# GpSimd and VectorE in program order: a two-layer graph kernel with its planner's order taken from two engines

## The chip, the cores and the metric

The kernel runs on one core of a Trainium2 chip. The core has four compute engines, each with an instruction queue that it works through in order: TensorE (PE in the profile) for matrix products, VectorE (DVE), ScalarE (ACT) and GpSimd (POOL). SyncE (SP) issues most of the DMAs. Engines wait for one another through semaphores. The metric is the time of one execution on the device in microseconds.

## The reference

A graph of 2708 nodes with 128 features and an adjacency matrix `adj` of which most entries are zero, since each node has a few neighbours and itself; each row is scaled to sum to 1. Two layers follow each other, each added to its input and normalized:

```python
x = _layernorm(x + _L0_gnn_ref(x, adj, W))       # hyperbolic mean over neighbours
x = _layernorm(x + _L1_gnn_ref(x, adj, ...))     # messages between neighbours

# layer 0
XW = mobius_matvec(W, X)
gamma = 2.0 / jnp.maximum(1.0 - jnp.sum(XW * XW, axis=-1, keepdims=True), EPS)
two_mean = (A_hat @ (gamma * XW)) / _clamp_abs(A_hat @ (gamma - 1.0))
...                                               # norms, artanh, tanh, relu
# layer 1
messages = gelu(s[:, None, :] + d[None, :, :] + msg_b)
aggregated = jnp.einsum('ijd,ij->id', messages, adj)
new_feats = concatenate([node_feats, aggregated]) @ upd_w.T + upd_b
h = gelu(new_feats) + node_feats                  # then a layer norm with ln_w, ln_b
```

Layer 0 needs products with the whole adjacency matrix. Layer 1 needs a gelu for each edge of the graph.

## The kernel before, in words

Nodes are cut into 22 blocks of 124 rows. The kernel goes through the following work, most of it overlapped.

**Products.** For each block, two halves of its adjacency columns are loaded (`aT`, L372, issued by SP). ACT turns them into signs (L375), DVE checks them against the diagonal (L378), and TensorE multiplies the signs with the prepared features (L397). DVE evacuates the sums (L413) and searches the packed words of the same product for the places of the neighbours (L431, L433). The sums stand in one of two PSUM banks called "op".

**Batches.** Blocks are grouped into seven batches. A batch turns the places into lists of edges: peeling the keys (L451 to L454), sorting (L493), counting (L506 to L527), places from a product with a triangular matrix (TensorE L523 and L524, DVE L536), a running sum (L538), a split into three parts that goes back and forth between ACT and DVE (L547, ACT L550, L554, ACT L555, L558), one-hot rows `R` (ACT L566, DVE L569), a selection by TensorE (L583), and the index `J` of the neighbour for each edge (L591 to L599).

**Epilogues.** Blocks are also grouped into five chunks (0 to 4, 5 to 8, 9 to 13, 14 to 18, 19 to 21). For a chunk, a chain of small DVE operations computes the factors of layer 0: L630, a power on POOL (L632), L641 to L669 with a logarithm and a tanh on ACT, then residual and statistics (L679 to L682), L685, a second power on POOL (L145), L689. Then each block is normalized (ACT L697, POOL L700), transposed (L702) and projected (L708, L709, into an "op" bank). The projection is written to a table in HBM (L716) and split into parts (ACT L315 and L317, DVE L316 and L318). Table 0 holds blocks 0 to 8, table 1 the others.

**Messages.** POOL gathers the neighbour's row from the table for 128 edges at a time (L342, an indirect DMA, four of them to a group `dd`, five groups buffered). DVE adds the own part (L765), ACT applies gelu (L766), TensorE sums by node (L778). A first pass uses table 0 (66 gathers), a second pass table 1 (41 gathers). In the second pass each finished block is updated (L817, L818, ACT L819), and groups of one to four blocks are normalized twice (`finish`: L828, L807 to L809, power on POOL L145, L834, L838, statistics and power again, L846, ACT L848) and stored.

**What sets the order.** The Python code does not emit stage after stage. The main loop over blocks emits loads, products and evacuations; beside it stand "threads", lists of small steps of batches, epilogues and the first message pass, each with a start and an end on a clock of blocks. After every main step `advance` emits the steps of each thread that have become due. The second message pass emits finish steps through `queue` and `drain`, one step of messages at a time. What is emitted is then handed to the scheduler of the language, which orders the instructions of each engine by its own estimate of when they are ready, taking the emission order as a priority. Each engine then issues in the order that results.

Of the kernel before, what the change touches and what calls it, by code (L numbers as in the profile page):

```python
# [10 lines left out]
F32 = mybir.dt.float32  # L11
U32 = mybir.dt.uint32
BF16 = mybir.dt.bfloat16
I32 = mybir.dt.int32
AF = mybir.ActivationFunctionType
OP = mybir.AluOpType
# [49 lines left out]
def hyperbolic_then_message_kernel(  # L66
# [148 lines left out]
    def cols(n, pool=sc, p=Q):  # L215
        count[0] += 1
        name = f"c{count[0]}" if count[0] < 100 else "k" + SHORT[count[0] - 101]
        return pool.tile([p, max(n, NB)], F32, name=name)[:, :n]
# [90 lines left out]
    def bank(name, bufs=2):  # L309
        return ps.tile([P, 512], F32, name=name, bufs=bufs)  # L310
# [51 lines left out]
    def signs_of(b):  # L362

        def load():
            dgb = stream.tile([P, Q], F32, name="dgb", bufs=2)
            nc.sync.dma_start(dgb, bass.AP(tensor=adj_r.tensor, offset=adj_r.offset + b * Q, ap=[[0, P], [1, Q]]))
            signs[b] = (stream.tile([Q, NB, Q], BF16, name="sgn"), dgb)

        def half(h):
            sgn, dgb = signs[b]  # L370
            aP = stream.tile([P, HALF, Q], F32, name="aT", bufs=3)
            nc.sync.dma_start(aP, adj_t[b, :, h * HALF : (h + 1) * HALF, :])  # L372
            aT = aP[:Q]
            at = 2 * b + h
            nc.scalar.activation(  # L375
                sgn[:, h * HALF : (h + 1) * HALF, :], aT.bitcast(U32), AF.Sign, accum_out=nn[:, at : at + 1]
            )
            nc.vector.scalar_tensor_tensor(  # L378
                aT,
                aT,  # L380
                1.0,
                dgb[:Q].unsqueeze(1).to_broadcast([Q, HALF, Q]),
                op0=OP.mult,
                op1=OP.is_equal,
                accum_out=ne[:, at : at + 1],
            )

        return [load, lambda: half(0), lambda: half(1)]

    def products(b):  # L390

        def part(j0, j1):
            if j0 == 0:
                sums[b] = bank("op")
            op, (sgn, _) = sums[b], signs[b]
            for j in range(j0, j1):
                nc.tensor.matmul(  # L397
                    op[:Q, :WIDE], lhsT=sgn[:, j, :], rhs=ym[:, j, :], start=(j == 0), stop=(j == NB - 1)
                )
                if j == 0:  # L400
                    nc.tensor.matmul(
                        op[:Q, KEYS:WIDE], lhsT=nidentb[:Q, :Q], rhs=ym[:, b, KEYS:], start=False, stop=False
                    )

        return [lambda: part(0, HALF), lambda: part(HALF, NB)]

    def evacuate(b):

        blocks, S = of_block[b]

        def first():
            op = sums[b]
            nc.vector.tensor_reduce(  # L413
                nom[:, b, :], op[:Q, :ONES].rearrange("p (g d) -> p d g", g=3), axis=AX.X, op=OP.add
            )
            nc.scalar.copy(cnt[:, b : b + 1], op[:Q, ONES : ONES + 1])  # L416
            if b == blocks[0]:
                if S:
                    v = small.tile([Q, len(blocks), S, 8], F32, name="v", bufs=2)
                    idx = small.tile([Q, len(blocks), S, 8], U32, name="idx", bufs=2)  # L420
                    slots[blocks] = (v, idx)
                else:
                    words = small.tile([Q, Q], F32, name="words")
                    nc.scalar.copy(words, op[:Q, KEYS:WIDE])
                    slots[blocks] = (words, None)
            if S:
                v, idx = slots[blocks]
                i = b - blocks[0]
                words = op[:Q, KEYS:WIDE]
                for s, (lo, hi) in enumerate(segments(S)):  # L430
                    nc.vector.max(v[:, i, s, :], words[:, lo:hi])  # L431
                for s, (lo, hi) in enumerate(segments(S)):
                    nc.vector.max_index(idx[:, i, s, :], v[:, i, s, :], words[:, lo:hi])  # L433

        def second():
            u = nom[:, b, :D]
            junk = row.tile([Q, D], BF16, name="junk")
            nc.scalar.activation(junk, u, AF.Square, accum_out=ss[:, b : b + 1])
            nc.scalar.activation(u, u, AF.Relu)
            junk = row.tile([Q, D], BF16, name="junk")  # L440
            nc.scalar.activation(junk, u, AF.Square, accum_out=us[:, b : b + 1])

        return [first, second]
# [369 lines left out]
    def update(agT, b, dgb):  # L813

        h = own1[:, b, :]
        up = bank("sel", SELS)
        nc.tensor.matmul(up[:Q, :D], lhsT=agT, rhs=wu2, start=True, stop=True)  # L817
        nc.vector.scalar_tensor_tensor(h, up[:Q, :D], dgb, h, op0=OP.mult, op1=OP.add)  # L818
        nc.scalar.activation(h, h, AF.Gelu)  # L819
# [104 lines left out]
    def advance(now):  # L924
        for t in threads:
            start, end, steps, done = t
            due = len(steps) if now >= end else int(len(steps) * max(0.0, now - start) / (end - start))
            while t[3] < due:
                steps[t[3]]()
                t[3] += 1  # L930
# [21 lines left out]
        thread(clock, clock + n * PACE, messages(0, range(b0, b1), kept))  # L952
        clock += n * PACE

    for i in range(NB + 1):
        main = []
        if i == 1:
            main.append(lambda: nc.sync.dma_start(x_all, x_p))
        if i < NB:
            main += signs_of(i)  # L960
        if i >= 1:
            main += products(i - 1)
            main += evacuate(i - 1)
        for k, step in enumerate(main):
            step()
            advance(i + (k + 1) / len(main))
    now = NB + 1.0
    late_at = max(t[1] for t in threads)
    while now < late_at:
        now = min(late_at, now + 0.05)  # L970
        advance(now)

    count[0] = 60
    bad = cols(4, p=Q)
    bp = bank("sel", SELS)
    nc.tensor.matmul(bp[:Q, :NL], lhsT=ones[:Q, :Q], rhs=deg, start=True, stop=True)
    over = cols(NL)
    nc.vector.tensor_tensor(over, bp[:Q, :NL], cap, op=OP.is_gt)
    nc.vector.tensor_reduce(bad[:, 0:1], over, axis=AX.X, op=OP.max)
    dz = cols(NB)  # L980
    cn = cols(4)
    nc.vector.tensor_scalar(dz, dg, 0.0, None, op0=OP.is_le)
    nc.vector.tensor_reduce(cn[:, 0:1], dz, axis=AX.X, op=OP.add)
    nc.vector.tensor_reduce(cn[:, 1:2], nn, axis=AX.X, op=OP.add)
    nc.vector.tensor_reduce(cn[:, 2:3], ne, axis=AX.X, op=OP.add)
    nc.vector.tensor_reduce(cn[:, 3:4], deg, axis=AX.X, op=OP.add)
    cp = bank("sel", SELS)
    nc.tensor.matmul(cp[:Q, :4], lhsT=ones[:Q, :Q], rhs=cn, start=True, stop=True)
    tot = cols(4)
    nc.scalar.copy(tot, cp[:Q, :4])  # L990
    pads = float(NP - N)
    nc.vector.tensor_scalar(bad[:, 1:2], tot[:, 0:1], pads, None, op0=OP.not_equal)
    nc.vector.tensor_scalar_add(tot[:, 2:3], tot[:, 2:3], -pads * NP)
    nc.vector.tensor_tensor(bad[:, 2:3], tot[:, 2:3], tot[:, 1:2], op=OP.not_equal)
    nc.vector.tensor_scalar_add(tot[:, 3:4], tot[:, 3:4], float(N))
    nc.vector.tensor_tensor(bad[:, 3:4], tot[:, 3:4], tot[:, 1:2], op=OP.not_equal)
    bsum = cols(1)
    nc.vector.tensor_reduce(bsum, bad, axis=AX.X, op=OP.add)
    flag = sc.tile([Q, 1], I32, name="flag")
    nc.vector.tensor_copy(flag, bsum)  # L1000

    queue = []
    groups = []
    at = 0
    for n in ENDS:
        groups.append(LATE_ORDER[at : at + n])
        at += n
    group_of = {b: g for g in groups for b in g}
    state = {}

    def ended(b, ag, at):
        agT = edge.tile([P, Q], F32, name="agT", bufs=4)
        nc.scalar.copy(agT, ag[:, :Q])
        bs = group_of[b]

        def up():
            update(agT, b, dg[:, b : b + 1])

        queue.append((at + 1, up))
        if b == bs[-1]:  # L1020
            for k in range(3):
                queue.append((at + 2 + k, lambda k=k: state.setdefault((bs[0], "f"), finish(bs))[k]()))

    def drain(now):
        due = [q for q in queue if q[0] <= now]
        queue[:] = [q for q in queue if q[0] > now]
        for _, f in due:
            f()

    for i, step in enumerate(messages(1, LATE_ORDER, ended)):  # L1030
        step()
        drain(i - (DDS - 2))
    drain(10**6)

    dense = nc.values_load(flag[0:1, 0:1], min_val=0, max_val=4)
    with tc.If(dense > 0):
# [123 lines left out]
```

## Time and profile before

| what | us |
|---|---|
| median of 3 runs | 466.12 (463.27 to 473.36) |
| the profiled execution, its own time | 462.5 |
| span of the profiled execution | 460.7 |
| DVE busy | 280.5 |
| PE busy | 278.5 |
| ACT busy | 233.8 |
| POOL busy | 175.8 |
| first gather from table 0 starts at | 185.85 |
| first gather from table 1 starts at | 360.32 |

A row of the timeline gives start and length in microseconds, the engine, the line of the kernel, the operation, output and inputs, shapes, and in brackets the idle time of the engine before it with what ended that time. "x3" merges neighbours of a kind. A row of the waits reads: engine, line and tile that waited, what it waited for, total microseconds, number of times, longest case. The names of tiles leave out buffer numbers.

### The profile page before, as it was taken

The page shows a single profiled execution, that of the slowest core. Times are in us where ns is not written, and L with a number is a line of the kernel's source. Part 1 is how long each engine was busy: PE and PEld are TensorE (multiplying, and loading weights), DVE is VectorE, ACT ScalarE, POOL GpSimd, SP SyncE. Part 2 cuts the span into 40 slices and gives each one's busy share as a digit, 9 for nine tenths or more (in the row PEclk, how much of TensorE's full clock was granted, in tenths as well). Part 3 has the DMA queues.
Part 4 walks back from the last instruction along what each step waited for, and adds up shares of the span by engine and source line. Part 5 has one row for each costly group of instructions (what it writes and reads, how often), then busy time and mean ns, then how long its engine had stood idle before and what let it go on. Part 6 is the DMA issues. An engine that isn't in the chain of part 4 may idle for free. (4 is left out here: it accounts for less than half of the span.)

```text
span 460.7 us, 6392 instructions
## 1 busy us (share of the span) xinstructions
PE 278.5 (60%) x1813; PEld 198.2 (43%) x1813; DVE 280.5 (61%) x1174; ACT 233.8 (51%) x647; POOL 175.8 (38%) x332
## 2 busy tenths in 40 slices
PE   3606948471789328966509578987089767556500
PEld 3603525240356114645308445855046656555400
DVE  3896898989717892355138553679286223338770
ACT  3764646366546756434028565677178333233520
POOL 9900000020401001677770770012724777782230
PEclk9855997975589858977758969999589896865755
DMA  7970444353234660163512351830100222121110
GB/s 185 369 192 1 127 126 130 82 174 127 67 90 162 159 187 23 43 234 112 175 43 74 102 144 36 207 110 11 46 25 24 62 52 53 48 55 40 37 33 15
DMA packets 20160, 45.86 MB, mean 100 GB/s; under 512 B 6185, under 2 KB 12517, under 8 KB 19861
## 3 DMA queue, kind: packets, MB, share of 16 engines
q1 hardware_dynamic: 15413, 37.75, 27.1%
q0 software_dynamic: 3424, 7.02, 6.0%
q10 hardware_dynamic: 1280, 0.60, 0.7%
q8 instruction: 16, 0.26, 0.3%
q14 instruction: 27, 0.22, 0.2%
HBM read 42.58 MB, written 2.78 MB: 98 GB/s over the span
## 5 line engine op out<-in xcount | busy, mean ns | idle before, releaser
L342 POOL DMA_INDIRECT dd<-table_dram,J x107 | 109.5, 1023 | 60.6 <-issue 27.9
L397 PE MATMUL op<-ym,sgn 124*124 124x512 bf16 x484 | 122.7, 407 | 12.1 <-DVE idx L433 11.6
L397 PEld LDWEIGHTS <-sgn 124*124 124x124 bf16 x484 | 67.8, 146 | 51.6 <-issue 21.8
L375 ACT ACTIVATE sgn<-aT 124x1364 bf16<-124x1364 uint32 x44 | 58.8, 1337 | 31.5 <-DMA aT<-in_adj_t_dram 13.5
L378 DVE SCALAR_TENSOR_TENSOR aT<-aT,dgb 124x1364 f32<-124x1364 f32 x44 | 69.1, 1573 | 4.7 <-ACT cnt L416 2.8
L778 PE MATMUL ag<-rw,ge 128*128 128x124 f32 x214 | 40.2, 322 | 17.2 <-ACT ge L766 17.1
L766 ACT ACTIVATE ge<-dd 128x512 f32<-128x512 f32 (+2 forms) x30 | 17.6, 586 | 52.0 <-DVE dd L765 50.9
L778 PEld LDWEIGHTS ag<-rw,ge 128*128 128x128 f32 x214 | 35.1, 232 | 18.4 <-ACT ge L766 18.0
L765 DVE TENSOR_TENSOR dd<-sel,dd 128x512 f32<-128x512 f32 (+2 forms) x30 | 18.8, 628 | 38.6 <-DMA dd<-table_dram,J 30.3
L632 POOL TENSOR_TENSOR knr<-knr,halves 124x10 f32<-124x10 f32 (+2 forms) x5 | 9.0, 1807 | 79.5 <-DVE knr L630 79.5
L753 PE MATMUL sel<-sl,R 124*128 124x128 bf16 x321 | 31.0, 244 | 12.1 <-DVE dd L765 5.9
L753 PEld LDWEIGHTS <-R 124*128 124x128 bf16 x321 | 25.9, 112 | 22.3 <-issue 19.8
L708 PE MATMUL op<-wall,x1T 128*124 128x512 f32 x44 | 30.4, 781 | 5.8 <-ACT gd L720 5.7
L566 ACT ACTIVATE r<-iota,mid 124x256 f32<-124x256 f32 (+4 forms) x48 | 24.0, 528 | 8.3 <-DVE R L569 7.7
L583 PE MATMUL sel<-zl,R 124*128 124x16 bf16 (+4 forms) x321 | 15.9, 183 | 19.1 <-DVE R L569 8.9
L520 POOL MEMSET rst<- 124x128 bf16 (+5 forms) x7 | 2.1, 294 | 63.8 <-DVE scan L538 61.4
L756 PE MATMUL rt<-identb,R 124*128 124x124 bf16 x107 | 16.5, 243 | 14.3 <-ACT rw L759 13.1
L583 PEld LDWEIGHTS <-R 124*128 124x128 bf16 x321 | 13.6, 101 | 24.4 <-DVE R L569 15.5
L145 POOL TENSOR_TENSOR rs<-rs,halves 124x4 f32<-124x4 f32 (+3 forms) x16 | 13.7, 860 | 25.4 <-DVE rs L809 25.3
L316 DVE TENSOR_TENSOR stmp<-op,sl 124x128 f32<-124x128 f32 x22 | 6.4, 289 | 25.1 <-ACT sl L315 25.1
L413 DVE TENSOR_REDUCE nom<-op 124x129 f32<-124x387 f32 x22 | 12.2, 553 | 14.6 <-PE op L397 14.6
L759 ACT CAST rw<-rt 128x496 f32<-128x496 bf16 (+2 forms) x30 | 15.7, 522 | 9.8 <-PE ag L778 7.7
(232 smaller groups left out, 596.1 us busy)
## 6 DMA issues: line engine op xcount, KB each, us to landing
aT<-in_adj_t_dram SPq DMA_DIRECT2D x44, 682.0 KB
dd<-table_dram,J POOLq DMA_INDIRECT x107, 2.6
x_sb<-in_x_p_dram SPq DMA_DIRECT2D x1, 1408.0 KB
own<-in_x_t_dram SPq DMA_DIRECT2D x1, 1364.0 KB
dgb<-in_adj_r_dram SPq DMA_DIRECT2D x22, 62.0 KB
table_dram<-d SPq DMA_DIRECT2D x22, 62.0 KB
out_dram<-own SPq DMA_DIRECT2D x21, 62.0 KB
mw<-in_L_gnn_msg_w_dram ACTq DMA_DIRECT2D x1, 128.0 KB
```

What stands on the lines that cost most here:

```text
L342: nc.gpsimd.indirect_dma_start(out=o, out_offset=None, in_=src, in_offset=bass.IndirectOffsetOnAxis(ap=at, axis=0))
L375: nc.scalar.activation(sgn[:, h * HALF : (h + 1) * HALF, :], aT.bitcast(U32), AF.Sign, accum_out=nn[:, at : at + 1])
L378: nc.vector.scalar_tensor_tensor(aT, aT, 1.0, dgb[:Q].unsqueeze(1).to_broadcast([Q, HALF, Q]), op0=OP.mult, op1=OP.is_equal, accum_out=ne[ ...
L397: nc.tensor.matmul(op[:Q, :WIDE], lhsT=sgn[:, j, :], rhs=ym[:, j, :], start=(j == 0), stop=(j == NB - 1))
L566: nc.scalar.activation(r0[:, : nt * P], iota[:Q, : nt * P], AF.Abs, scale=2.0, bias=st["mid"][:, at : at + 1])
L583: nc.tensor.matmul(sp[:, q, :], lhsT=R[:, t, :], rhs=st["zl"][:, h, k, i, :], start=(h == 0), stop=(h == 2))
L708: nc.tensor.matmul(dp[:Q, :], lhsT=st[b], rhs=wall.rearrange("p a d -> p (a d)"), start=True, stop=False)
L753: nc.tensor.matmul(X[:, i, :], lhsT=R[:, t, :], rhs=sl[:, b, h, :], start=(h == 0), stop=(h == 2))
L756: nc.tensor.transpose(RT[:, i, :Q], R[:, t, :], identb[:Q, :Q])
L765: nc.vector.tensor_tensor(dd[:, :w, :], X[:, :w, :], dd[:, :w, :], op=OP.add)
L766: nc.scalar.activation(ge[:, :w, :], dd[:, :w, :], AF.Gelu)
L778: nc.tensor.matmul(ag[:, :Q], lhsT=ge[:, i, :], rhs=rw[:, i, :], start=False, stop=is_last)
```

## The change

The part of the program from the main loop to the end of the second message pass is put into a block that tells the language to keep the emitted order for two engines:

```diff
-    for i in range(NB + 1):
-        main = []
...
-        for k, step in enumerate(main):
-            step()
-            advance(i + (k + 1) / len(main))
...
-    for i, step in enumerate(messages(1, LATE_ORDER, ended)):
-        step()
-        drain(i - (DDS - 2))
-    drain(10**6)
+    with tc.manual_schedule(engines={mybir.EngineType.Pool, mybir.EngineType.DVE}):
+        for i in range(NB + 1):
+            main = []
...
+            for k, step in enumerate(main):
+                step()
+                advance(i + (k + 1) / len(main))
...
+        for i, step in enumerate(messages(1, LATE_ORDER, ended)):
+            step()
+            drain(i - (DDS - 2))
+        drain(10**6)
```

Everything between the shown lines is indented and otherwise unchanged. Within the block POOL and DVE issue in the order in which the Python code emits. TensorE, ACT and SP are still ordered by the scheduler, which now takes the given order of the other two into account, so their orders change as well. The preparation ahead of the main loop is emitted outside the block.

## The prediction

> **What bounds the kernel now.** I read the page's head first. VectorE (DVE) and TensorE are each busy for three fifths of the span and no engine more, so the end is set by waits between engines; the chain that ended last is spread over all of them.
>
> ```profile
> span 460.7 us, 6392 instructions
> PE 278.5 (60%) x1813; PEld 198.2 (43%) x1813; DVE 280.5 (61%) x1174; ACT 233.8 (51%) x647; POOL 175.8 (38%) x332
> POOL 9%; PE 9%; DVE 7%; issue 5%; DMA 4%; ACT 3%; POOLq 0%; ACTq 0%; DVEq 0%
> ```
>
> Next the busy time in windows of 23 us (columns: window, length, then busy us of each engine). From 46 to 115 us DVE is busy for 91 to 93% of each window: there DVE itself is the bound. From 115 to 360 it is not. In the tail, 414 to 437, it is at 19 of 23 again.
>
> ```profile
> 46.00:69.00 23.00, 16.11 (x78) 9.82 (x76) 20.85 (x102) 13.31 (x34) 0.12 (x1) 0.98 0.46 127
> 92.00:115.00 23.00, 9.88 (x56) 6.35 (x57) 21.29 (x125) 14.72 (x34) 3.13 (x5) 0.65 0.46 151
> 414.00:437.00 23.00, 13.93 (x75) 12.32 (x74) 19.00 (x95) 10.83 (x33) 6.14 (x7) 0.65 0.13 38
> ```
>
> Then the waits (us in total, times, longest). Few of DVE's waits are on ScalarE (ACT), though its chains run through ACT at every step: the present order puts other work there. Two are on GpSimd (POOL), each with one very long case.
>
> ```profile
> DVE ktn L641 <- POOL knr L632: 21.0, 4, 17.5
> DVE knm L689 <- POOL krs L145: 17.1, 4, 8.4
> DVE c L269 <- ACT c L268: 0.3, 1, 0.3
> ```
>
> The timeline shows what those cases are. The power L632 was ready when L630 ended (218.3), but stood on POOL behind a run of gathers (L342, one every 1.25 us) until 235.7; DVE had L641 next in its queue and stood still, and ACT and TensorE with it. The same happens at 259.9 (6.8 us) and 324.2 (8.4 us) with L145. These three **hold-ups** are 32.8 us.
>
> ```profile
> 218.09 0.17 DVE L630 TENSOR_SCALAR knr<-sp 124x10 f32<-124x10 f32 x1
> 234.78 0.94 POOL L342 DMA_INDIRECT dd<-table_dram,J  x1 [0.30 <-issue]
> 235.74 2.00 POOL L632 TENSOR_TENSOR knr<-knr,halves 124x10 f32<-124x10 f32 x1
> 237.78 0.17 DVE L641 TENSOR_TENSOR ktn<-kq,knr 124x5 f32<-124x5 f32 x1 [17.54 <-POOL knr L632]
> 266.75 0.17 DVE L689 SCALAR_TENSOR_TENSOR knm<-mv,krs 124x5 f32<-124x5 f32 x1 [6.83 <-POOL krs L145]
> 332.54 0.17 DVE L689 SCALAR_TENSOR_TENSOR knm<-mv,krs 124x5 f32<-124x5 f32 x1 [8.37 <-POOL krs L145]
> ```
>
> The last price I need is that of a DVE instruction right behind the one it depends on. Three links of the series L230 take 0.62 us, so 0.21 each; an independent neighbour starts 0.06 to 0.07 after the one before it (L655, then L659).
>
> ```profile
> 27.84 0.62 DVE L230 SCALAR_TENSOR_TENSOR c<-c,c 124x22 f32<-124x22 f32 x3
> 154.64 0.14 DVE L655 SCALAR_TENSOR_TENSOR kp<-kp,kzz 124x4 f32<-124x4 f32 x1
> 154.70 0.16 DVE L659 TENSOR_SCALAR km<-kz 124x4 f32<-124x4 f32 x1
> ```
>
> **The change part by part.** No arithmetic, load or buffer changes; the order on DVE and POOL does, and the orders of TensorE and ACT shift with it. I compared the issue orders of the two built programs. (Lines from 955 on are one higher in the new file; I use the old numbers.)
>
> *DVE chains become neighbours.* The present order deals two or three chains like cards (L655, L506, L655, L507). The emitted order runs each step of a chain whole. Pairs in which an instruction directly follows one whose result it uses grow from 131 to 398: 72 more between the first L413 and the seventh, 38 more from there to the first L765, 95 more up to the flag, 63 more in the tail. A narrow pair costs 0.21 - 0.07 = 0.14. On 124x124 words it is 0.12 (L451 to L452: 50.00 to 50.26 as neighbours, 54.05 to 54.19 with L431 between). On wide operations the pause hides better; I set 0.05 as the low end. I take 0.12.
>
> *DVE waits for ACT and TensorE lie bare.* In a batch, L547, L554 and L558 now follow one another, each needing an ACT copy of the one before (L550 0.61, L555 0.63 us for the first batch; 0.28 and 0.29 for the next). L433, L569 and L378 covered them. Floor: the copies, 1.2 us; ceiling: with an L375 (1.34 us) ahead of L550 on ACT, 2.6. I take 1.9 for the first batch, 0.8 to 1 for others, and 0.9 a time for L536 behind TensorE's L523/L524, the one such wait shown today.
>
> Stage by stage:
> - 46 to 115 us, DVE-bound: 72 x 0.12 = 8.6, and 3.5 of bare waits: **+12** (5 to 15). Nothing covers it.
> - 115 to 186, up to the first gather: 38 x 0.12 = 4.6, and some 3 of waits; DVE is busy for 43 of 69 us, so about half is covered: **+4** (0 to 8).
> - 186 to 360: 95 x 0.12 = 11.4 and three batches at 1: **+14** (7 to 17). Half might fall into waits for gathers (L765, 30.3 us in all), hence the 7.
> - The hold-ups: the power for blocks 9 to 13 now stands behind 28 gathers instead of 37: 9 x 1.25 = 11 less. Both L145 powers now stand ahead of the eight and the ten gathers that held them; what is left is the power itself, 1.2 us and its handover: 6.8 + 8.4 becomes about 3, 12 less. **-23** (-30 to -12). The gathers pushed back find POOL idle soon after (276 to 305).
> - Late chain: today L630 of blocks 19 to 21 runs 0.1 us after L689 of blocks 14 to 18 (332.62), and that chain overlaps the five projections (L316/L318, 337.7 to 347.7). In the new order DVE does all five projections, then the evacuation L413 of block 21, and only then L630. With block 21's sums still holding one of the two "op" banks, projections run at 2.2 to 3.3 us instead of the 1.7 to 2 seen at 341 to 346: 11 to 16 us. Eight gathers (10 us) also stand ahead of this L632 on POOL, beside the projections. What waits is the last table, and so every late gather: **+15** (8 to 20).
> - Tail: powers at 410.0 and 413.6 are stuck behind gathers and cost DVE 4.85 and 2.26 us. The new order puts powers ahead of the last five gathers (-7); these gathers end some 3 us later, but the last L765 already waits until 428 for DVE, so this is hidden. Against it: L807 and L808 alternate in bare pairs, 63 x 0.12 = 7.6, of which I count 5 since some lie inside waits for POOL. **-2** (-7 to +6).
>
> Sum: 12 + 4 + 14 - 23 + 15 - 2 = **+20**. On the profiled execution's own time (462.5 us: span 460.7 and 1.8 around it) this gives 482.5; I say **482**. The median of the runs shown is 466.1 and the three spread from 463 to 473, so about 2% is all that can be told from no change here.
>
> The Trainium skill, "SBUF — State Buffer", section "Summary: rules for kernel authors", says that a GpSimd operation reading SBUF and a VectorE operation with two SBUF inputs block each other fully. The trace speaks against it at one place: L632 ran from 332.87 to 334.18, and inside it DVE ran L452 and L454, two SBUF inputs each, at 0.17 and 0.18 us. By the rule the powers moved beside busy DVE work would add up to 2 us each, some 6 for three; by this row nothing.
>
> **The rivals.**
> 1. *The hold-ups decide* (other side: faster). They are the only places where all engines stand at once, and an in-order DVE elsewhere may only shift its pauses into waits that exist anyway. If half of the 30 us of new pauses (12 + 4 + 14) is hidden, the late chain costs its low end, and tail and hold-ups give -5 and -25: 15 + 8 - 5 - 25 = -7, 455; with pauses at their low ends (5 + 0 + 7) and the late chain covered, -18, 444. I put it at **449**. It decides from the point at which the pauses add under 10 us. Against it: from 46 to 115 us DVE has under 10% slack.
> 2. *Gain and cost cancel.* Pauses at 18, late chain at 10, hold-ups -23, tail -2: +3, **466**.
> 3. *A new hold-up.* L632 of blocks 19 to 21 behind its eight gathers, not covered by the projections, because these gathers wait for the L700 ahead of them, and L378 in fixed places holds back the adjacency loads: +10 and +8 on the forecast, **500**.
> 4. *Nothing happens*, the orders being nearly the same: excluded by the count of pairs; only POOL's order is similar.
>
> **How the numbers follow.** Forecast (470 to 492 by itself) 0.50; first rival 0.20; second 0.20; third 0.10. The range leaves out the lower half of rival 1 and part of rival 3: 449 to 500. Faster by over 2% (under 457) takes rival 1: 0.20. Within 2% (457 to 475) takes rival 2 and the low edge of the forecast: 0.24. Slower: 0.56.
>
> **What would show it.** Right: L413 of the seventh block, today at 109.3, lies 8 to 15 us later; new waits of DVE L554, L558 and L536 on ACT; the longest wait for L632 at 5 to 10 us instead of 17.5, those for L145 in L689 under 3; the first table_1 gather (360.3) at about 380; from there to the end some 98 us. Wrong: DVE's busy time unchanged at 280 with no new waits on ACT (then rival 1), or the late L630 as early as today.

## The result, and the profile after

The changed kernel is slower: 503.51 us (median of 4, 498.60 to 504.86) against 464.69 us (median of 4, 463.01 to 473.36) on the same chip, a ratio of 1.084 with a 95% interval of 1.075 to 1.093. Its profiled execution has a span of 496.8 us, 36.1 more than before. The forecast was 482.

The head of its page: the work is the same but for a few instructions, and DVE is busy for 18.3 us more with the same 1174 instructions.

```profile
span 496.8 us, 6403 instructions
...
PE 288.0 (58%) x1813; PEld 204.5 (41%) x1813; DVE 298.8 (60%) x1174; ACT 241.1 (49%) x648; POOL 169.7 (34%) x332
```

The same windows as before the change (window, length, busy us of each engine). Between 46 and 115 us DVE was busy for 20.9 to 21.3 of each 23 us; now it has 16.6 to 19.3, and the stretch reaches to 138.

```profile
46.00:69.00 23.00, 16.40 (x79) 10.04 (x77) 19.25 (x92) 11.34 (x27) 0.00 (x0) 0.99 0.41 114
69.00:92.00 23.00, 11.91 (x104) 8.84 (x105) 16.55 (x51) 11.60 (x27) 0.31 (x2) 0.71 0.28 78
...
115.00:138.00 23.00, 2.39 (x37) 2.01 (x37) 18.88 (x88) 10.76 (x23) 0.40 (x1) 0.50 0.32 95
```

The waits of DVE over the whole span (total, times, longest). L632 is down from 21.0 to 7.6 and L689 from 17.1 to 2.1: the hold-ups behind gathers have gone as far as forecast. Two of the three longest are waits on ACT: that of L316 was the second longest before (25.1 us, 17 times, longest 4.4), that of L431 did not exist before, and I had named neither as a wait.

```profile
DVE stmp L316 <- ACT sl L315: 40.8, 16, 7.0
DVE dd L765 <- DMA dd<-table_dram,J: 23.0, 8, 4.4
DVE v L431 <- ACT cnt L416: 14.6, 21, 3.2
...
DVE ktn L641 <- POOL knr L632: 7.6, 1, 7.6
...
DVE knm L689 <- POOL krs L145: 2.1, 2, 1.1
```

In the timeline (start, length, engine, line, and in brackets the idle time before it), the L641 that had waited 17.54 us and the L689 of chunk 3 that had waited 8.37:

```profile
245.96 0.17 DVE L641 TENSOR_TENSOR ktn<-kq,knr 124x5 f32<-124x5 f32 x1 [7.62 <-POOL knr L632]
...
347.70 0.15 DVE L689 SCALAR_TENSOR_TENSOR knm<-mv,krs 124x5 f32<-124x5 f32 x1
```

To find where the time came from I use seven marks in the timeline: the first L413, the L689 of each of the five chunks, the end. All later tables do the same, because the part ahead of the first L413, which no edit here touches, takes 47 us in some executions and 53 to 55 in others (the changed kernel itself had 47.3 in its first profile and 53.9 in a second). Lengths in us between the marks:

| kernel | L413 to chunk 0 | to 1 | to 2 | to 3 | to 4 | to the end | sum |
|---|---|---|---|---|---|---|---|
| before | 72.1 | 54.0 | 93.7 | 65.8 | 13.9 | 114.3 | 413.7 |
| after | 92.2 | 53.3 | 86.6 | 68.3 | 38.7 | 110.4 | 449.5 |
| difference | +20.1 | -0.7 | -7.1 | +2.5 | +24.8 | -3.9 | +35.8 |

So the loss sits in two places, the first stretch and the last chunk's chain; the gain between chunks 1 and 2 is small.

### The profile page after: what moved, and what is told of

It is laid out like the page before. It is cut to its first block, busy times and chain, and to the rows that moved or that the text cites. A ratio compares the mean times of both kernels' runs of the same rounds, so it can differ in the third digit from the quotient of the medians.

```text
span 496.8 us, 6403 instructions
## 1 busy us (share of the span) xinstructions
PE 288.0 (58%) x1813; PEld 204.5 (41%) x1813; DVE 298.8 (60%) x1174; ACT 241.1 (49%) x648; POOL 169.7 (34%) x332
## 4 chain that ended last, share of the span: by engine, by line
DVE 33%; PE 23%; ACT 13%; POOL 12%; issue 10%; DMA 6%; POOLq 0%; ACTq 0%; DVEq 0%; SPq 0%
POOL dd L342 10%; PE op L397 9%; DVE aT L378 7%; PE op L708 4%; DMA aT<-in_adj_t_dram 3%; ACT sgn L375 3%; PE ag L778 3%; DVE st L807 2%; DVE R L569 2%; DVE mv L808 2%; DVE st L681 1%; DMA own<-in_x_t_dram 1%; DVE own L838 1%; POOL rs L145 1%; ACT r L566 1%
## 5 line engine op out<-in xcount | busy, mean ns | idle before, releaser
L397 PE MATMUL op<-ym,sgn 124*124 124x512 bf16 x484 | 123.1, 408 | 21.3 <-DVE idx L433 21.3
L342 POOL DMA_INDIRECT dd<-table_dram,J x107 | 106.9, 999 | 41.9 <-issue 32.1
L397 PEld LDWEIGHTS <-sgn 124*124 124x124 bf16 x484 | 68.5, 147 | 63.0 <-ACT junk L441 18.7
L375 ACT ACTIVATE sgn<-aT 124x1364 bf16<-124x1364 uint32 x44 | 58.8, 1336 | 57.0 <-DMA aT<-in_adj_t_dram 38.1
L378 DVE SCALAR_TENSOR_TENSOR aT<-aT,dgb 124x1364 f32<-124x1364 f32 x44 | 68.7, 1572 | 2.6 <-ACT sgn L375 1.6
L778 PE MATMUL ag<-rw,ge 128*128 128x124 f32 x214 | 43.0, 346 | 24.6 <-ACT ge L766 17.3
L778 PEld LDWEIGHTS ag<-rw,ge 128*128 128x128 f32 x214 | 37.1, 249 | 27.7 <-ACT ge L766 19.6
L753 PE MATMUL sel<-sl,R 124*128 124x128 bf16 x321 | 32.5, 247 | 17.6 <-DVE own L818 11.1
L145 POOL TENSOR_TENSOR krs<-krs,halves 124x5 f32<-124x5 f32 (+2 forms) x5 | 5.4, 1087 | 103.9 <-DVE krs L685 103.9
L632 POOL TENSOR_TENSOR knr<-knr,halves 124x10 f32<-124x10 f32 (+2 forms) x5 | 9.0, 1799 | 86.7 <-DVE ka L631 86.7
L583 PE MATMUL sel<-zl,R 124*128 124x16 bf16 (+4 forms) x321 | 17.7, 195 | 35.1 <-DVE R L569 35.1
L766 ACT ACTIVATE ge<-dd 128x512 f32<-128x512 f32 (+2 forms) x30 | 17.3, 583 | 41.0 <-DVE dd L765 38.1
L753 PEld LDWEIGHTS <-R 124*128 124x128 bf16 x321 | 26.5, 114 | 24.5 <-issue 22.7
L765 DVE TENSOR_TENSOR dd<-sel,dd 128x512 f32<-128x512 f32 (+2 forms) x30 | 18.8, 630 | 27.5 <-DMA dd<-table_dram,J 23.0
L708 PE MATMUL op<-wall,x1T 128*124 128x512 f32 x44 | 30.6, 786 | 4.4 <-ACT gd L720 4.4
L583 PEld LDWEIGHTS <-R 124*128 124x128 bf16 x321 | 15.6, 112 | 40.5 <-DVE R L569 38.2
L316 DVE TENSOR_TENSOR stmp<-op,sl 124x128 f32<-124x128 f32 x22 | 6.4, 290 | 41.3 <-ACT sl L315 40.8
L759 ACT CAST rw<-rt 128x496 f32<-128x496 bf16 (+2 forms) x30 | 15.7, 524 | 23.2 <-PE rt L756 13.9
L413 DVE TENSOR_REDUCE nom<-op 124x129 f32<-124x387 f32 x22 | 12.2, 555 | 12.9 <-PE op L397 12.9
L569 DVE TENSOR_SCALAR R<-r,dflat 124x256 bf16<-124x256 f32 (+4 forms) x48 | 16.0, 359 | 3.9 <-ACT r L566 3.7
```

The source lines that it names most:

```text
L145: nc.gpsimd.tensor_tensor(o, v, halves[:Q, k : k + 1].to_broadcast([Q, v.shape[1]]), op=OP.pow)
L342: nc.gpsimd.indirect_dma_start(out=o, out_offset=None, in_=src, in_offset=bass.IndirectOffsetOnAxis(ap=at, axis=0))
L375: nc.scalar.activation(sgn[:, h * HALF : (h + 1) * HALF, :], aT.bitcast(U32), AF.Sign, accum_out=nn[:, at : at + 1])
L378: nc.vector.scalar_tensor_tensor(aT, aT, 1.0, dgb[:Q].unsqueeze(1).to_broadcast([Q, HALF, Q]), op0=OP.mult, op1=OP.is_equal, accum_out=ne[ ...
L397: nc.tensor.matmul(op[:Q, :WIDE], lhsT=sgn[:, j, :], rhs=ym[:, j, :], start=(j == 0), stop=(j == NB - 1))
L569: nc.vector.tensor_scalar(R[:, t0 : t0 + nt, :].rearrange("p t e -> p (t e)"), r0[:, : nt * P], st["dflat"][:, at : at + 1], -0.5, op0=OP. ...
```

## The experiments

Theory A after the result: VectorE's fixed order is the whole cost, in the first stretch (pauses and bare waits) and in the late chain (five projections ahead of it); GpSimd's fixed order is a gain. Every edit below is to the changed kernel. The marks of all runs, as above:

| kernel | to chunk 0 | to 1 | to 2 | to 3 | to 4 | to the end | sum |
|---|---|---|---|---|---|---|---|
| GpSimd only | 72.2 | 52.4 | 77.9 | 57.3 | 28.4 | 107.2 | 395.4 |
| VectorE only | 91.6 | 53.3 | 92.9 | 71.8 | 45.5 | 116.1 | 471.2 |
| from block 7 on | 74.3 | 53.2 | 86.6 | 68.3 | 38.5 | 110.8 | 431.7 |
| projections between | 91.5 | 53.4 | 85.8 | 68.6 | 30.1 | 108.2 | 437.6 |
| projections behind | 91.5 | 53.4 | 85.8 | 68.6 | 20.0 | 114.8 | 434.1 |
| evacuation first | 91.7 | 53.3 | 86.5 | 68.2 | 31.1 | 110.6 | 441.5 |
| counts later | 90.7 | 54.1 | 84.5 | 67.3 | 39.0 | 110.5 | 446.1 |
| GpSimd only, projections behind | 72.2 | 50.7 | 77.2 | 57.7 | 15.5 | 111.8 | 385.0 |

### One engine at a time

```diff
-    with tc.manual_schedule(engines={mybir.EngineType.Pool, mybir.EngineType.DVE}):
+    with tc.manual_schedule(engines={mybir.EngineType.Pool}):
```

> Only GpSimd in the emitted order, VectorE in the scheduler's order again. Theory A (VectorE's fixed order is what costs: about 20 us in the stretch from 46 us to chunk 0 and about 25 us in the chain of the last chunk; GpSimd's fixed order gives back hold-ups): the losses go and the gain stays, the two stalls of 17.5 and 8.4 us behind gathers shrink to under 8 us together, so faster than the kernel before, about 447 us (438 to 456). Rival B (GpSimd's fixed order is a cost too, since gathers that could go early now wait behind small operations that are not ready): 470 us or more, and the first gather of table_1 later than the 360.3 us of before. Rival C (the hold-ups were cover for other work, and nothing comes of them): 462 to 468 us, the stalls shorter and other waits in their place.

Measured: 449.46 us (442.32 to 452.17), where the kernel before took 461.07 to 475.62 beside it; the fastest of each are 18.8 us apart, and from the first L413 it is 18.3 us less than before. As theory A said; rivals B and C fall. The second run has `DVE` in the place of `Pool`:

> Only VectorE in the emitted order, GpSimd in the scheduler's order. Theory A: all of the loss and none of what GpSimd's order gives back, so no faster than the changed kernel: 505 to 525 us, chunk 0's last wait for its power at about 139 us, and again waits of over 10 us for a power that stands behind gathers. Rival B: if GpSimd's order costs, clearly faster than the changed kernel, under 490 us.

Measured: 527.35 us (526.01 to 528.25), 2 us above the forecast's upper end. Both times GpSimd's order gives back about 20 us (413.7 - 395.4 = 18.3; 471.2 - 449.5 = 21.7), and both times VectorE's costs some 55 (57.5 and 54.1). The two nearly add: the change is a sum of a gain and a loss nearly three times as large. (The loss takes in what the scheduler then does with the orders of ACT, TensorE and SP; no run fixes those.)

The hold-ups themselves show what the gain is worth. With GpSimd alone, the way from chunk 1 to 3 is 24.3 us shorter than before (15.8 + 8.5). With VectorE's order also fixed, the same change of GpSimd's order shortens it by 9.8 (6.3 + 3.5). Two rows of the timeline of the VectorE-only run say why:

```profile
257.58 0.17 DVE L641 TENSOR_TENSOR ktn<-kq,knr 124x5 f32<-124x5 f32 x1 [13.86 <-POOL knr L632]
...
363.28 0.17 DVE L689 SCALAR_TENSOR_TENSOR knm<-mv,krs 124x5 f32<-124x5 f32 x1 [3.10 <-POOL krs L145]
```

A VectorE that arrives later stands shorter behind the same gathers: 13.9 and 3.1 us where it was 17.5 and 8.4, and the 6.8 of chunk 2 is gone.

### The first stretch

```diff
-    with tc.manual_schedule(engines={mybir.EngineType.Pool, mybir.EngineType.DVE}):
-        for i in range(NB + 1):
+    def blocks_of(start, end):
+        for i in range(start, end):
...
+    blocks_of(0, 7)
+    with tc.manual_schedule(engines={mybir.EngineType.Pool, mybir.EngineType.DVE}):
+        blocks_of(7, NB + 1)
```

> The first seven steps of the block loop (blocks 0 to 6 of the adjacency, with what is emitted beside them) are left to the scheduler; from the eighth step on both engines take the emitted order. Theory A: the 20 us that chunk 0 loses are lost by VectorE's fixed order in this stretch and stay lost to the end, so chunk 0's last operation on VectorE (the mean of its norm) comes at 119 to 124 us in place of 139.5, and the end is 14 to 22 us sooner than the changed kernel's: about 485 us (480 to 492). Rival D (a later stage would have waited anyway, on adjacency loads or on the loop of products, so the early loss is not on the path): chunk 0 sooner, but the end within 6 us of the changed kernel's, 497 to 505 us.

Measured: 487.50 us (486.65 to 487.83). Chunk 0 comes 74.3 us after the first L413 (the clock times in the expectation assumed the shorter start), 17.9 sooner, and all of it stays to the end: 17.8. The first stretch is fully on the path; rival D falls.

What is in the 20.1 us? The trace accounts for it. DVE's busy time there goes from 67.4 to 74.6 us (+7.2), its waits for ACT from 2.5 in 3 cases to 14.8 in 18 (+12.3), its waits for others from 1.8 to 0.5, and gaps too short to be labelled from 0.3 to 2.3. The number of instructions is the same (317 and 318), so I read the busy time as the price of dependent neighbours, which overlap less. In these rows L681 starts 0.38 us behind the L679 that it reads, L682 0.33 behind L681 (they are from the timeline of the run with the projections between; the changed kernel has the same figures). Before the change an independent neighbour mostly started 0.25 behind L679 and 0.20 behind L681.

```profile
376.46 0.34 DVE L679 SCALAR_TENSOR_TENSOR nom<-nom,kh,x_sb 124x128 f32<-124x128 f32 x1
376.84 0.29 DVE L681 BATCH_NORM_STATS2 st<-nom 124x6 f32<-124x128 f32 x1
377.17 0.18 DVE L682 BATCH_NORM_AGGREGATE mv<-st 124x2 f32<-124x6 f32 x1
```

To see whether such pauses are on the path, the three operations were emitted one block apart:

```diff
             V.scalar_tensor_tensor(u, u, c("h")[:, b - b0 : b - b0 + 1], x_sb[:, b, :], op0=OP.mult, op1=OP.add)
-            s6 = row.tile([Q, 6], F32, name="st")
-            V.bn_stats(s6, u)
-            V.bn_aggr(mv[:, b, :], s6)
+            if b > b0:
+                stats(b - 1)
+            if b > b0 + 1:
+                aggr(b - 2)
+            if b == b1 - 1:
+                stats(b)
+                aggr(b - 1)
+                aggr(b)
...
```

> The changed kernel with the three VectorE operations of each block's residual (L679, L681, L682, each reading the one before) emitted one block apart, so that neighbours are of different blocks. In the changed kernel L681 starts 0.38 us behind the L679 that it reads, where behind an independent one the next starts after 0.25; L682 0.33 behind L681 against 0.20. So some 34 pairs at 0.13 us. Theory A (pauses of dependent neighbours are on the path wherever VectorE is what bounds): 3 to 4.5 us sooner to the end. Rival J (VectorE waits for ScalarE, GpSimd or TensorE soon after in any case and the pauses vanish in that wait): less than 1.5 us sooner.

This one was run beside the changed kernel itself:

> The changed kernel itself, beside the others. The first profile of it had its first L413 at 47.3 us; every kernel run since had it at 53.0 to 54.4 us, whatever its order. If that difference lies ahead of the changed part, the first L413 comes here at 53 to 54 us or at 47, and from it to the end 449 to 451 us in either case, with 92, 53, 87, 68 and 39 us between the marks. If the difference belongs to the edits, the first L413 is at 47.3 us again and the end at 496 to 498 us.

Measured: the changed kernel 534.19 us, this edit 528.68, the kernel before 482.04, on a chip where all three are slower than elsewhere (the ratio of after to before is 1.105 there, 1.098 to 1.111). In the timeline of the changed kernel there, DVE and ACT stand for up to 24 us at a time until something arrives from a queue that the profile doesn't name, and meanwhile products of TensorE follow each other only every 0.7 us or later, without a wait that the profile shows:

```profile
233.61 0.38 PE L397 MATMUL op<-ym,sgn 124*124 124x512 bf16 x1 [0.36 <-issue]
...
234.32 0.38 PE L397 MATMUL op<-ym,sgn 124*124 124x512 bf16 x1 [0.34 <-issue]
...
253.54 0.56 DVE L413 TENSOR_REDUCE nom<-op 124x129 f32<-124x387 f32 x1 [21.61 <-remote]
```

These stalls begin only where gathers run (most of their time stands before L759, L765, L413 and L1014), and the sum is 480.2 where 449 to 451 was expected. Late gathers alone don't explain them: neither L413 nor the products L397 ahead of it read gathered rows. What holds them stays open. So of these two runs only the stretches ahead of the gathers are compared: 92.1 us to chunk 0 and 53.2 to chunk 1 for the changed kernel (92.2 and 53.3 in its first profile), 90.7 and 52.7 with the edit, 1.9 us less. The nine blocks of these chunks have 18 such pairs, 18 x 0.13 = 2.3 us. But four edits that change nothing in what VectorE is given ahead of chunk 0 (VectorE only, projections between, projections behind, evacuation first) reach it after 91.5 to 91.7 us as well, 0.4 to 0.7 before the changed kernel. So 1.2 to 1.9 of the 2.3 us are the edit's own: in these stretches the pauses are on the path for more than half of their price, which fits theory A. What the other pairs are worth later on was not measured. The first L413 of the changed kernel, here at 53.9 us, settles the other point: the longer start belongs to no edit.

For the waits on ACT, look at one in the timeline of the changed kernel. L536 needs L534, and L534 a product (L524) that begins at 102.66; but on ACT a whole L375 stands ahead of L534, and that L375 itself had waited 1.40 us for an adjacency load:

```profile
102.13 0.29 DVE L527 SCALAR_TENSOR_TENSOR cm<-col,m 124x128 f32<-124x128 f32 x1
...
103.07 1.34 ACT L375 ACTIVATE sgn<-aT 124x1364 bf16<-124x1364 uint32 x1 [1.40 <-DMA aT<-in_adj_t_dram]
...
104.41 0.24 ACT L534 ACTIVATE mid<-sel,ones 124x2 f32<-124x2 f32 x1
...
104.68 0.16 DVE L536 TENSOR_TENSOR m<-m,sel 124x2 f32<-124x2 f32 x1 [2.26 <-ACT mid L534]
```

Three more waits of the stretch, L554 (2.18), L569 (2.24) and L431 (2.01), have an L375 ahead of the answer in the same way. Three edits were each to take one possible cause away.

The counts (which L431 waits for) copied later:

```diff
                 nom[:, b, :], op[:Q, :ONES].rearrange("p (g d) -> p d g", g=3), axis=AX.X, op=OP.add
             )
-            nc.scalar.copy(cnt[:, b : b + 1], op[:Q, ONES : ONES + 1])
...
                     nc.vector.max_index(idx[:, i, s, :], v[:, i, s, :], words[:, lo:hi])
+            nc.scalar.copy(cnt[:, b : b + 1], op[:Q, ONES : ONES + 1])
```

> The changed kernel with one step moved: ScalarE's copy of each block's counts (L416), which reads the same PSUM bank as VectorE's maxima, is emitted behind the maxima and their indices instead of between the block's reduction (L413) and the first maximum (L431). Theory A (in a fixed order VectorE waits 14.6 us in 21 places for this copy, before the change nowhere, and most of that is on the path): from the first L413 to the end 449.5 us become 437 to 443, the wait before L431 goes to nothing, and the end is 7 to 13 us sooner than the changed kernel's. Rival H (VectorE waits there for something that comes a little later anyway, and the next wait takes it over): less than 4 us sooner, other waits of VectorE longer by about 10 us.

Measured: 502.09 us (495.38 to 506.20), 446.1 from the first L413: 3.4 sooner, not 7 to 13. The 14.6 us of waits before L431 are gone, and the next waits have taken most of it, as rival H said (L378 on L375 from 1.6 to 6.2 us, L630 on L441 from 1.3 to 4.7, L671 on L670 from 5.3 to 7.2). In the first stretch 92.2 became 90.7, against 91.5 to 91.7 in edits that do not touch it.

A fourth buffer for the adjacency (`aT`, 3 to 4; `DDS` 5 to 3 and `agT` 4 to 2 to make room):

> The changed kernel with a fourth buffer for the adjacency halves (aT); to make room the groups of gathered rows have three buffers in place of five and agT two in place of four, which changes VectorE's and GpSimd's order only behind chunk 1, so this run is read from the first L413 to chunk 1 alone. In the changed kernel ScalarE stands 28.7 us before L375 for adjacency loads between the first L413 and chunk 0 (7.9 us before the change), since L378 frees their buffers late, and VectorE's answers stand behind that L375. Theory K (this loop is part of chunk 0's 20 us): with one more buffer the loads come earlier, ScalarE's waits for them fall below 15 us, and chunk 0 is reached 84 to 88 us after the first L413 in place of 92.2. Rival L (the loads are late as a consequence only; VectorE's pauses and its waits for the length of L375 itself make the 20 us): 90.5 to 92.5 us, whatever ScalarE waits.

Measured: chunk 0 after 91.7 us. ACT's waits for loads fall only from 28.7 to 24.8 us, where theory K asked for less than 15, and VectorE's waits for ACT stay (14.6). The time is rival L's, but the edit did not take the cause away. In both kernels a load is issued 0.1 us behind the L378 that VectorE has just ended, at nearly the same times after the first L413 (62.5 and 62.1 us in these rows: first the changed kernel, then this edit):

```profile
109.66 0.08 DVE L378 DVE_READ_ACCUMULATOR aT<-aT,dgb 124x1 f32 x1
...
109.77 0.33 SPq L372 DMA_DIRECT2D aT<-in_adj_t_dram  x1
```

```profile
115.69 0.08 DVE L378 DVE_READ_ACCUMULATOR aT<-aT,dgb 124x1 f32 x1
...
115.81 0.33 SPq L372 DMA_DIRECT2D aT<-in_adj_t_dram  x1
```

ACT is one adjacency half further on, but it begins the sign ahead of that L534 55.4 us after the first L413 where it was 55.8, with the answer behind it as before. So VectorE sets when the loads come, and what it would be worth to have them early was not measured.

The sign cut into three:

```diff
-    nn = const.tile([Q, 2 * NB], F32, name="nn")
+    nn = const.tile([Q, 6 * NB], F32, name="nn")
...
-            nc.scalar.activation(
-                sgn[:, h * HALF : (h + 1) * HALF, :], aT.bitcast(U32), AF.Sign, accum_out=nn[:, at : at + 1]
-            )
+            for k, (lo, hi) in enumerate(((0, 4), (4, 8), (8, HALF))):
+                nc.scalar.activation(
+                    sgn[:, h * HALF + lo : h * HALF + hi, :],
+                    aT[:, lo:hi, :].bitcast(U32),
+                    AF.Sign,
+                    accum_out=nn[:, 3 * at + k : 3 * at + k + 1],
+                )
```

> The changed kernel with ScalarE's sign of an adjacency half (L375, 1.34 us and 0.19 us for its sum) cut into three of 4, 4 and 3 blocks, so that a small answer for VectorE can be issued between them; VectorE's and GpSimd's orders stay. In the changed kernel VectorE waits 14.8 us for ScalarE between the first L413 and chunk 0 (2.5 us before the change), and in the four longest of these waits (2.18, 2.24, 2.26 and 2.01 us) one whole L375 stands ahead of the answer. Theory M (the length of L375 ahead of the answer is what these waits are made of): the four fall to 0.8 to 1.5 us each, the sum to 10 to 12 us, and chunk 0 is reached 87.5 to 90.5 us after the first L413 in place of 92.2. Rival N (the answers are late because ScalarE itself gets its inputs late, or the pieces fill the gaps again): four waits of about 2 us as before, 91.5 us or more.

Measured: chunk 0 after 90.9 us, between the two; the whole was 526.55 us, on a second chip with such stalls (the kernel before 482.28, a ratio of 1.090, 1.079 to 1.102). The four waits became 0.70, 1.65, 2.01 and 2.18 (timeline of this kernel, whose lines here are four higher, L376 being the sign):

```profile
79.81 0.71 DVE L558 TENSOR_TENSOR cm<-scan,zl 124x528 f32<-124x528 f32 x1 [0.70 <-ACT zl L554]
...
109.48 0.62 ACT L376 ACTIVATE sgn<-aT 124x496 bf16<-124x496 uint32 x1 [1.27 <-DMA aT<-in_adj_t_dram]
...
110.97 0.16 DVE L540 TENSOR_TENSOR m<-m,sel 124x2 f32<-124x2 f32 x1 [2.01 <-ACT mid L538]
```

The length of L375 made one wait and part of a second; in the two others ACT itself stands in front of an adjacency load (1.27 us here, 2.64 for the last) with the answer queued behind. So no one cause of the 12.3 us was found: the later counts gave 1.5 us and the cut sign 1.3, of which edits that do not touch the stretch also show 0.4 to 0.7, and the fourth buffer left the sign where it was. Which share ScalarE's order has in it, and which the loads, stays open. Fixing ScalarE's order as well was not tried.

### The last chunk's chain

The last six steps of blocks 14 to 18 (normalize and project) get a place of their own on the clock:

```diff
-        thread(clock, clock + span, epilogue(b0, b1))
+        steps = epilogue(b0, b1)
+        if b0 == 14:
+            thread(clock, clock + span * 15 / 21, steps[:15])
+            thread(NB + 1.0, NB + 1.9, steps[15:])
+            ends.append(NB + 1.0)
+            clock += span
+            continue
+        thread(clock, clock + span, steps)
```

> Both engines in the emitted order as in the changed kernel, but the five projections of blocks 14 to 18 are emitted between the steps of the last chunk's chain, not ahead of it. Theory A (the five projections, one after another, stand on VectorE ahead of the last chunk's first operation and hold it back): the stretch from the end of chunk 3's norm to that of chunk 4's falls from 38.7 us to 15 to 22 us, and the end is 15 to 24 us sooner, about 484 us (478 to 490). Rival E (the last chain is long by its own dependent steps in a fixed order, or by the projections' one PSUM bank wherever they stand): the stretch stays at 30 us or more and the end within 8 us of the changed kernel's, 495 to 505 us.

Measured: 491.34 us (489.86 to 492.61), 11.9 sooner from the first L413; the stretch is 30.1. Neither side has it all: the stretch is at rival E's edge, the end sooner than E's 8 us and later than theory A's 15. L630 did start 20.6 us sooner (301.6 after the first L413 for 322.2), but the chain from there to L689 then took 27.8 us in place of 16.9: the projections cost VectorE their time between its steps as well. With the last six steps at `NB + 2.3`, behind the chain:

> Both engines in the emitted order, the five projections of blocks 14 to 18 emitted behind the whole chain of the last chunk. Theory A (five projections cost the last chain what they take on VectorE, wherever they stand before its end): the stretch from chunk 3's norm to chunk 4's falls to 16 to 20 us, where it was 38.7 with the projections ahead of the chain and 30.1 with them between its steps; eight projections then follow at 1.3 to 1.8 us each, so the first gather of table_1 comes some 18 us behind that norm, where it was 11.7, and the end is 10 to 16 us sooner than the changed kernel's. Rival I (the last chain is slow by its own dependent steps in a fixed order): the stretch stays above 24 us and the end is no sooner than with the projections between the steps, 437.5 us from the first L413.

Measured: 490.45 us (489.00 to 492.42); the stretch is 20.0 and the sum 15.4 less. Eight projections then follow, the first gather of table_1 comes 15.9 us behind the norm (11.7 before the edit), and a part of the gain goes there: 18.7 less became 15.4. Rival I falls. The stretch is still 6.1 us longer than the 13.9 before the change; that rest was not taken apart.

Why do five projections take from 347.70 to 367.41? In the timeline of the changed kernel each product L708 begins when ACT has read the last quarter (L720) of the projection before:

```profile
354.57 0.28 ACT L720 ACTIVATE gd<-op 124x128 f32<-124x128 f32 x1
354.90 1.75 PE L708 MATMUL op<-wall,x1T 128*124 128x512 f32 x2 [1.20 <-ACT gd L720]
...
363.77 0.29 DVE L316 TENSOR_TENSOR stmp<-op,sl 124x128 f32<-124x128 f32 x1 [2.29 <-ACT sl L315]
...
366.73 0.29 DVE L316 TENSOR_TENSOR stmp<-op,sl 124x128 f32<-124x128 f32 x1 [2.01 <-ACT sl L315]
...
367.59 0.55 DVE L413 TENSOR_REDUCE nom<-op 124x129 f32<-124x387 f32 x1
...
369.45 0.17 DVE L630 TENSOR_SCALAR knr<-sp 124x6 f32<-124x6 f32 x1 [0.38 <-ACT junk L441]
```

Before the change the third and fourth of them stood 1.7 us apart, and ACT was not waited for:

```profile
342.72 0.27 DVE L316 TENSOR_TENSOR stmp<-op,sl 124x128 f32<-124x128 f32 x1
...
344.41 0.28 DVE L316 TENSOR_TENSOR stmp<-op,sl 124x128 f32<-124x128 f32 x1
```

In the changed kernel the other bank holds block 21 until L413, L431 and L433 from 367.59 on, which VectorE has in its queue behind all five. If that is the reason, it is enough to emit these three ahead of the projections:

```diff
-                advance(i + (k + 1) / len(main))
+                if i < NB or k + 1 == len(main):
+                    advance(i + (k + 1) / len(main))
```

> The changed kernel with VectorE's evacuation of the last block (L413, L431, L433 of block 21) emitted ahead of the five projections of blocks 14 to 18 instead of behind them; the projections stay ahead of the last chunk's chain. Theory F (the projections take 3.0 to 5 us each because block 21's products hold one of the two banks of their pool, so each waits for ScalarE's last copy of the one before): with both banks they take 1.3 to 2 us each as before the change, the stretch from the end of chunk 3's norm to that of chunk 4's falls from 38.7 us to 28 to 33 us, and the end is 6 to 10 us sooner. Rival G (they are slow because ScalarE's five operations and its table load stand one behind the other for each of them, whichever bank): the stretch stays at 36 us or more, the end within 3 us of the changed kernel's.

Measured: 493.99 us (490.73 to 496.94); the stretch is 31.1 and the sum 8.0 less, as theory F said. From the second projection on the L316 now follow one another at 1.3 to 1.8 us (timeline of this run):

```profile
364.15 0.29 DVE L316 TENSOR_TENSOR stmp<-op,sl 124x128 f32<-124x128 f32 x1 [0.37 <-ACT sl L315]
...
365.74 0.29 DVE L316 TENSOR_TENSOR stmp<-op,sl 124x128 f32<-124x128 f32 x1 [0.64 <-ACT sl L315]
```

### A version that beats both

With GpSimd's order alone the last stretch was 28.4 us, longer than before the change (13.9). There, in the timeline of that run, the power of the last chunk stood behind the additions L700 and eight gathers, from 314.6 to 327.6:

```profile
314.58 0.15 DVE L630 TENSOR_SCALAR knr<-sp 124x6 f32<-124x6 f32 x1
...
327.61 1.36 POOL L632 TENSOR_TENSOR knr<-knr,halves 124x6 f32<-124x6 f32 x1
...
329.00 0.16 DVE L641 TENSOR_TENSOR ktn<-kq,knr 124x3 f32<-124x3 f32 x1 [4.84 <-POOL knr L632]
```

So the projections are again emitted behind the last chunk's chain (`NB + 2.3`), with GpSimd alone in the emitted order.

> GpSimd alone in the emitted order, VectorE in the scheduler's, and the projections of blocks 14 to 18 emitted behind the last chunk's chain, so that on GpSimd the last chunk's power (L632) stands ahead of the additions of chunk 3 and of eight gathers. With GpSimd's order alone that power waited 13 us behind them (given at 260.2, begun at 273.2 us after the first L413). If that wait is on the path: the last chunk's norm ends at 272 to 280 us after the first L413 in place of 288.2, and the kernel is 6 to 12 us faster than with GpSimd's order alone, about 440 us (434 to 445). If the projections, now later, are what table_1 waits for in any case: within 4 us of it.

Measured: 441.34 us (440.36 to 443.21), where the kernel before took 461.41 to 473.01 beside it, so the slowest run is 18.2 us under the fastest of before. The last stretch is 15.5 us and the sum 10.4 less than with GpSimd's order alone. The edit moves the projections as well as L632, so the 10.4 us are the two together. In its timeline L632 begins 0.2 us after L630:

```profile
312.47 0.15 DVE L630 TENSOR_SCALAR knr<-sp 124x6 f32<-124x6 f32 x1
...
312.70 1.32 POOL L632 TENSOR_TENSOR knr<-knr,halves 124x6 f32<-124x6 f32 x1 [0.62 <-DVE knr L630]
```

## Why the prediction was right and wrong, by its steps

The side was right and the amount was not: +36.1 us of span for the +20 worked out; the median of 503.51 us lies above the range's upper end of 500.

| step | forecast | measured |
|---|---|---|
| 46 to 115 us | +12 | +20.1 (to chunk 0) |
| up to the first gather | +4 | -0.7 (chunk 0 to 1) |
| 186 to 360, hold-ups | +14 - 23 = -9 | -4.6 (chunk 1 to 3) |
| late chain | +15 | +24.8 (chunk 3 to 4) |
| tail | -2 | -3.9 (chunk 4 to the end) |

Two terms carry the miss: the first stretch is 8.1 us dearer than forecast and the late chain 9.8, and the errors of the other three (4.4 dearer, 4.7 and 1.9 cheaper) nearly cancel, which is luck.

- **First stretch: the term of the bare waits was mis-sized.** Dependent neighbours were put at 8.6 us, and DVE's busy time grew by 7.2: that price held (0.13 a pair where 0.12 was taken, and at 124x128 too, so it did not hide better on wide operations). The bare waits were put at 3.5 and measured 12.3. I had priced a wait by the answer itself (0.28 to 0.63 us of copy) and had named an L375 ahead of it only as a ceiling for one case; it was there in four, at 2.0 to 2.3 us each. And L431, 14.6 us over the whole span, was missing from my list: I looked for chains of DVE alone and passed over L413, ACT's L416 and L431, three readers of one bank. The Trainium skill ("PSUM — Partial Sum Buffer", "PSUM bank collisions raise a hardware error") says that two engines must be kept from one bank even where both only read, and that a compiler adds a dependency for it; the trace agrees, in each of the 21 blocks that have an L431 it began only after a wait for L416, though it uses nothing that L416 writes. The forecast's reading that few of DVE's waits are on ACT was wrong before the change already: L316 and L318 waited 25.1 and 6.9 us for it. L413 of the seventh block came 28 us later, not 8 to 15; part of that is order, since chunk 0's L689, 9.7 us behind it before, is 2.0 behind it now.
- **Up to the first gather: too high by 4.7.** The stretch from chunk 0 to 1 lost nothing, and DVE's busy time in it is 35.7 us for 36.7, so next to nothing of the pauses shows, where I had counted half (taking such pairs apart still gave 0.5 us here).
- **Hold-ups: right in the trace, wrong in what they are worth.** The waits shrank as named (one case of 7.6 us for the 5 to 10, L689 under 1.2), and where VectorE keeps the scheduler's order the gain up to chunk 3 is 24.3 us for the 23. Together with VectorE's order it is 9.8. I subtracted a gain measured with an early VectorE from a kernel with a late one. (The three waits before the change add up to 32.7 us, not 32.8.)
- **186 to 360: +14** was mid-way: VectorE's order costs 5.2 us from chunk 1 to 3 with GpSimd free and 19.7 with GpSimd fixed.
- **Late chain: right cause, too small.** 15 forecast, 24.8 measured. The five projections on one bank ahead of L630 are shown by two runs (evacuation first: 7.6 less; projections behind: 18.7 less); the last 6.1 us were not taken apart. The first of them also waits for a table load on ACT (1.28 us at 353.28), and each took 3.0 to 5.1 us where I had 2.2 to 3.3.
- **Tail:** from the first gather of table_1 to the end 98.7 us, for "some 98"; the gather itself came at 398.1, not at about 380.
- **Rival 3** had a true mechanism: L632 stood behind L700 and eight gathers for 13 us, and taking that away, with the projections moved too, gave 10.4 us, but only with VectorE in the scheduler's order (10.4 is the difference of the two runs with GpSimd's order alone). In the changed kernel the projections cover it (POOL had been idle for 8.73 us when L632 began at 369.71). Its other half, the late adjacency loads, did show (ACT's waits for them went from 13.5 to 38.1 us), with VectorE's L378 setting when they are issued; what they cost was not measured, since the fourth buffer did not bring them sooner.
- **Rivals 1 and 2** rested on pauses that vanish in other waits. They nearly did from chunk 0 to 1, and not in the first stretch, as the count of busy time had said.

The rule of the Trainium skill ("SBUF — State Buffer", "Summary: rules for kernel authors") by which a GpSimd operation and a two-input VectorE operation block each other fully is not seen after the change either: in the timeline an L378, which reads two tiles in SBUF, lies wholly inside a power and takes 1.55 us, where its mean is 1.57.

```profile
107.81 2.00 POOL L632 TENSOR_TENSOR knr<-knr,halves 124x10 f32<-124x10 f32 x1 [37.27 <-DVE ka L631]
...
108.18 1.55 DVE L378 SCALAR_TENSOR_TENSOR aT<-aT,dgb 124x1364 f32<-124x1364 f32 x1
```

## What to carry to other kernels

In this kernel a fixed order paid on an engine whose few, short operations release others and stand behind long ones (GpSimd, 18 to 22 us), and cost on one that is busy for three fifths of the span and talks to every other at each step (VectorE, 54 to 58 us); take the engines one by one. When an order lays a wait bare, price it by what stands ahead of the answer in the answering engine's queue, not by the answer. And a gain read from a wait before the change holds only while the waiting engine arrives as early as it did.

## What the runs showed of the hardware

Two things I had not expected. Ahead of the gathers the marks of the changed kernel repeat to 0.1 us in its two profiles (92.2 and 92.1, 53.3 and 53.2), though edits that leave the first of these stretches alone moved it by 0.4 to 0.7. And on two of the chips engines stood for up to 24 us at a time where gathers run, in the changed kernel and in two edits of it, without a cause that the profile shows; the kernel before took 482 us there for 465 to 472 elsewhere.
